# The block products of a fused attention kernel's projections change places, and loads within its attention are spread or moved behind it

## The chip, the cores and the metric

The kernel runs on one core of a Trainium2 chip. A core has a tensor engine (PE) for matrix products, a vector engine (DVE), a scalar engine (ACT), a general engine (POOL) and a queue engine (SP) from which nearly all transfers (DMA) are issued in order. Products go to PSUM, everything else lives in SBUF. The metric is the time of one execution on the device in microseconds. The kernel before took a median of 3309.8 us in three runs (3304.54 to 3311.78).

## The reference, cut to what matters

The input `x` is 8 images of 512 channels by 1024 positions, in float32. Two layers follow each other for each image:

```python
# layer 0, per image: 8 heads of 64 channels
hn  = group_norm(x, gn1)                       # 32 groups
q, k, v = split(w_qkv @ hn + b_qkv)
a   = softmax((q * s) @ (k * s)) @ v           # s = 64 ** -0.25, 1024 x 1024 per head
x1  = x + group_norm(w_proj @ a + b_proj, gn2)
# layer 1, per image: one head of 512 channels, weights normalized by rows
q, k, v = split(w1_qkv @ x1 / rms)             # rms over all 1536 channels of a position
h   = softmax(q.T @ k * 512 ** -0.5) @ v
out = (x1 + w1_out @ h) * 2 ** -0.5
```

Everything is computed in float32. The change touches layer 0 alone: the projections to q and k, and the loads that run during its attention.

## The kernel before, in words

**The loop.** `for b in range(B)` runs over the eight images, called batches here. In each, the attention of layer 0 has 32 steps: four pairs of heads (`j`), and for each pair eight blocks of 128 query rows. Step `i` does this, in `Heads.step`: the row maxima (DVE) and exponentials (ACT) of the scores made before; every second step the product of the probabilities with v (`values`, tile `po`) for two row blocks that lie some steps back; a piece of projection for the next pair (`fill`); the scores of step `i + 1` (`scores`, tile `s`); the transpose of the probabilities of step `i - 1` (`turn`: a DVE transpose from `p` to `pb`, then four transfers of 256 KB from `pb` to `pT`[...]); and the scaling of this step's probabilities on POOL (`scale`). What a step has in `later` follows at the end, among it the additions on POOL that belong to the projection piece (`due`, and those put off by a step, `rest`). So the scores of the first block of a pair are made at the end of the last step of the pair before, and need that pair's q and k by then. `pb`, `p` and the projected pairs `qk` have two buffers each, the scores three in PSUM, and the small products (`po` and the projection pieces) share two PSUM banks.

After the loop comes the drain: the last two `values`, the output projection with its weights `proj7`, the second group norm, and layer 1, which begins with a product with `gram` and reads `x`. In layer 1 the weights product has four units of seven products (`weight_unit`); the sums for the next batch's projection are made between them.

**The projection with seven products.** For pairs 1 to 3 of the batches 1 to 7 (21 times) q and k come from `project_seven`: q and k of both halves of the positions are a 2 by 2 block product, and are computed with seven block products in place of eight, as in Strassen's method in Winograd's form. The sums on the side of the activations are made once for each batch by `Sums`, in the tiles `t24` and `t31` (which lies in the buffer `v_`) and in `hn` itself; those on the side of the weights at the start by `operands_qk`, into `far["qk7"]` in DRAM, from which `fetch_qk` brings a pair's share (896 KB). Each block product is 64 rows deep in four chunks; those of the upper and the lower 64 rows run side by side on PE. `pieces` makes them in four pieces, one in every second step: the first with two chunks (the seventh product, divided over the two halves), the other three with four. ACT evacuates the two PSUM banks of a piece (to `q1`, `q2`, `k1`, `k2`, the halves of q and k, or to three temporaries `tmp`), and the list `adds` says what POOL adds after each piece, in the same step and one step later. For batch 0, and for pair 0 of each batch, `project_qk` or `project_rows` makes the eight products.

**Order.** `InOrder` keeps every instruction in the program's order on its engine; nothing is rescheduled. A step that waits holds up everything behind it on its engine. All instructions carry the line of that helper, so the profile is read by tiles. `Slots` hands out seven buffers of 16 KB a partition in the order in which they come free.

**Loads within attention.** With `i` the step, all on SP's queue between the transfers of `pT`: at 8 and 16 the weights of pair 3 and of the next batch's pair 0 (`fetch_qk`), at 21 `gram` (1 MB; in the last batch `proj`), at 24 `v` (1 MB, weights of layer 0), and at the ends of the steps 25 to 28 the four parts of `x` (512 KB each). `t24`, `gram` and `proj` share a buffer. POOL applies the first norm to the next batch's `hn` at the ends of the steps 1, 3, 5 and 7 (`norm1.apply`), in batches 1 to 6.

Of the kernel before, what the change touches and what calls it, by code (L numbers as in the profile page):

```python
# [10 lines left out]
AF = mybir.ActivationFunctionType  # L11
ALU = mybir.AluOpType
AX = mybir.AxisListType
P = 128
# [38 lines left out]
def attention_blocks_kernel(  # L53
# [29 lines left out]
    CI, NT, HN = C // P, N // P, N // 2  # L83
# [66 lines left out]
    def load_x(b, xt, ci):  # L150
        SY.dma_start(out=xt[:, ci, :], in_=xv[b, :, ci, :])
# [6 lines left out]
    rows = const.tile([GQKV, P], F32, name="rows")  # L158
# [31 lines left out]
    bkq = const.tile([P, CI], F32, name="bkq")  # L190
# [16 lines left out]
    def rsqrt(r, v, n, name):  # L207
# [43 lines left out]
    def fetch(name, b):  # L251
        SY.dma_start(out=place(name, b), in_=far[name])
# [98 lines left out]
    NB = N // P  # L351
    STEPS, LAG = CI * NB, 5
    halves = (slice(0, D), slice(D, P))
# [63 lines left out]
    class Sums:  # L417
# [2 lines left out]


        def __init__(self, b, hn):
            self.hn, self.t24, self.t31 = hn, place("t24", b), near["v_"].rearrange("p (ci n) -> p ci n", ci=CI)

        def steps(self):
            hn, t24, t31, (up, low) = self.hn, self.t24, self.t31, halves
            t1, t2 = slice(0, HN), slice(HN, N)
            SY.dma_start(out=t31[up], in_=hn[low, :, t2])
            yield
            for ci in range(CI):  # L430
                VE.tensor_sub(t31[up, ci], t31[up, ci], hn[up, ci, t2])
                yield
            for ci in range(CI):
                VE.tensor_add(t24[up, ci], t31[up, ci], hn[up, ci, t1])
                yield
            SY.dma_start(out=t24[low], in_=t24[up])
            for ci in reversed(range(CI)):
                VE.tensor_sub(hn[up, ci, t2], hn[up, ci, t2], hn[up, ci, t1])
                if ci == 2:
                    SY.dma_start(out=t31[low, :2], in_=hn[up, 2:, t2])  # L440
                yield
            for ci in range(CI):
                VE.tensor_sub(t24[low, ci], hn[low, ci, t1], t24[low, ci])
                yield

        def right(self, half, k):

            hn, t24, t31, rows = self.hn, self.t24, self.t31, halves[half]
            group, ci = divmod(k, CI)
            if group == 0:  # L450
                return hn[rows, ci, :HN]
            if group == 1:
                return t24[rows, ci]
            if half:
                return hn[rows, ci, HN:] if group == 2 else t31[rows, ci]
            return t31[rows, ci] if group == 2 else hn[rows, ci, HN:]

    def project_seven(b, j, right):

        qk = pair.tile([P, 2, N], F32, tag="qk", name=f"qk_{b}_{j}")
        kp = qk[:, 1, :].rearrange("p (be m) -> p be m", be=4)
        w, tmp = near["qk7"][:, (j - 1) % 2], [near["v#"][:, k * HN : (k + 1) * HN] for k in range(3)]

        def turned(t):
            return t.rearrange("p (m be) -> p be m", be=4)

        q1, q2 = (qk[:, 0, th * HN : (th + 1) * HN] for th in range(2))
        k1, k2 = (kp[:, :, th * P : (th + 1) * P] for th in range(2))  # L470

        def add(to, a, b_):
            return lambda: PO.tensor_add(to, a, b_)

        adds = (
            ([add(tmp[1], tmp[1], tmp[0])], []),
            ([], []),
            ([add(q2, q2, q1), add(k1, k1, turned(q2))], [add(q1, q1, tmp[0]), add(tmp[1], tmp[1], q2)]),
            ([add(k1, k1, k2), add(k2, k2, turned(tmp[1]))], [add(q2, tmp[1], tmp[2])]),
        )  # L480

        def pieces():
            for n, group in enumerate((3, 0, 1, 2)):
                pms = [bank(f"pq7_{b}_{j}_{n}_{r}") for r in range(2)]
                lo, hi = CI * group, min(CI * group + CI, 14)
                for k in range(lo, hi):
                    for r in range(2):
                        PE.matmul(pms[r], w[halves[r], k, :], right(r, k), start=(k == lo), stop=(k == hi - 1))
                if n == 0:
                    AC.copy(tmp[1], pms[0])  # L490
                elif n == 1:
                    AC.activation(q1, pms[0], AF.Identity, bias=bqs[:, j : j + 1])
                elif n == 2:
                    AC.copy(q2, pms[0])
                else:

                    AC.activation(k2, turned(pms[0]), AF.Identity, bias=bkq[:, j : j + 1])
                AC.copy(*((tmp[0], pms[1]), (tmp[0], pms[1]), (k1, turned(pms[1])), (tmp[2], pms[1]))[n])
                yield adds[n]

        return qk, pieces()
# [193 lines left out]
    class Seven:  # L695
# [8 lines left out]
        half, drains = None, []  # L704
# [310 lines left out]
    gram = place("gram", 0)  # L1015
# [6 lines left out]
    def operands_qk():  # L1022

        (up, low), q, k = halves, near["qk"][:, 0], near["qk"][:, 1]
        s = big("s_qk", 2 * CI)
        s1, s2 = s[up, :CI, :], s[:, CI:, :]
        s3 = block.tile([P, CI, C], F32, tag="pb", name="s3_qk")[up]
        SY.dma_start(out=far["qk0"], in_=near["qk"][:, :, :, :P])
        SY.dma_start(out=s1, in_=k[low])
        PO.tensor_add(s1, k[up], s1)  # L1030
        PO.tensor_sub(s2[up], s1, q[up])
        PO.tensor_sub(s3, q[up], k[up])
        SY.dma_start(out=s2[low], in_=s2[up])
        PO.tensor_sub(s2[low], q[low], s2[low])
        for rows, lo, hi, src in (
            (slice(0, P), 0, 4, q), (low, 4, 8, k[low]), (up, 4, 8, s2[up]), (up, 8, 12, s3), (up, 12, 14, s1[:, :2]),
            (low, 12, 14, s1[:, 2:]), (low, 8, 12, s2[low]),
        ):
            SY.dma_start(out=far["qk7"][rows, lo:hi, :], in_=src[:, :, P:])

# [34 lines left out]
    norm1 = Norm1(0, x0)  # L1075
# [22 lines left out]
    woT, proj = done2[:, :CI, :], done2[:, CI:, :]  # L1098
# [43 lines left out]
    heads, norm1, hn_next = Heads(0, x0, v0_0, qk0), None, None  # L1142
# [3 lines left out]
    for b in range(B):  # L1146
        hn, more = heads.hn, b + 1 < B
        todo, due, rest = iter(()), [], []
        for i in range(STEPS):
            j, r = divmod(i, NB)  # L1150
# [10 lines left out]
            early, later = [], []  # L1161
            if i < CI:
                fill, later = fills[i] + fill, laters[i]
# [9 lines left out]
                        todo = project_out_half(b, heads, o_last)  # L1173
            later.append(lambda: [f() for f in due])

            if b and more and i % 2 and i < 2 * CI:
                later.append(lambda: norm1.apply(i // 2, PO))
            if not b:


                if i == CI:
                    hn_next = big(f"hn_{b + 1}")
                    norm1 = Norm1(b + 1, hn_next)
# [15 lines left out]
                fetch_qk(CI - 1, b)  # L1199
            if b and i == 2 * NB and more:  # L1200
                fetch_qk(CI, b)
            if b and i == STEPS - NB - 3:
                fetch("gram" if more else "proj", b)
            if b and i == STEPS - NB and more:
                near["v"] = near["v_"].rearrange("p (ci c) -> p ci c", ci=CI)
                SY.dma_start(out=near["v"], in_=far["v"])

            if i == STEPS - NB + 1:
                xt = big(f"x_{b}")
            if 0 <= i - (STEPS - NB + 1) < CI:  # L1210
                later.append(lambda: load_x(b, xt, i - (STEPS - NB + 1)))
            heads.step(i, fill, early, later)

        if more:
# [4 lines left out]
        heads.turn()  # L1219
        if more:  # L1220
            fetch("proj7", b)
            ta = big(f"ta_{b}").rearrange("p (k i) (h n) -> p k i h n", k=2, h=2)
            rhs = RightSide(heads.a, ta[:, 0], ta[:, 1])
            for j in range(CI // 2 + 1):
                rhs.sums(j)
            for _ in range(3):
                next(v0)
        else:
            fetch("score", b)
            begun = OutBegun(b, heads)  # L1230
        heads.values(STEPS // RG - 1)
        slots.give(f"v0_{b}")
        if more:
# [84 lines left out]
```

## Time and profile before

| what | before |
|---|---|
| median of three runs | 3309.8 us (3304.54 to 3311.78) |
| profiled execution: time, span | 3305.3 us, 3303.5 us |
| PE busy (matmul) | 3242.3 us, 98% |
| DVE, POOL, ACT busy | 2235.7, 1129.4, 1064.0 us |
| granted PE clock | 0.997 |
| transfers `pb` to `pT` | 1024 of 256 KB, 4.6 us to landing (median) |
| attention of batch 2 (908 to 1090 us) | PE busy 176.2, DVE 147.1, POOL 109.1, ACT 92.8 us; DMA 0.79 busy, 214 GB/s |

The profile is of one execution. Busy times are sums of instructions of an engine; a matmul's end is modelled. A wait is written "engine tile <- releasing engine tile": the idle time of the first before an instruction on its tile, and who ended it. A name such as `po<-pT,v` is a group of instructions that write `po` and read `pT` and `v`. In the profile's names `tmp` appears as `v` (it lies in the same buffer as v), `t31` too, and `tt` are the reciprocal row sums.

### The profile page before, as it was taken

What the parts mean: (1) busy time and instruction counts of PE and PEld (TensorE: products, weight loads), DVE (VectorE), ACT (ScalarE), POOL (GpSimd) and SP (SyncE); (2) the same over time, 40 slices, a digit from 0 to 9 for tenths busy, and PEclk for the clock granted to TensorE, in tenths of its full rate; (3) what the DMA queues carried; (4) which work ended last, traced back from release to release, by engine and by line L of the source; (5) the groups of instructions that cost most, each with busy time, mean ns of one, the idle gap of its engine ahead of it and who ended that gap; (6) DMA issues with size and microseconds to landing.
All of it is one profiled execution on the core that took longest, in us unless ns stands there. A gap on an engine that the chain in (4) does not pass through costs nothing.

```text
span 3303.5 us, 35734 instructions
## 1 busy us (share of the span) xinstructions
PE 3242.3 (98%) x13010; PEld 1597.1 (48%) x13010; DVE 2235.7 (68%) x2982; ACT 1064.0 (32%) x1813; POOL 1129.4 (34%) x945
## 2 busy tenths in 40 slices
PE   8999999999999999999999999999999999999899
PEld 5444544445444454444544445444454445444354
DVE  5696667855688556885668756686566866668653
ACT  2453114521155211551215412254122531245210
POOL 0552125611266012650227503264033631246111
PEclk9999999999999999999999999999999999999899
DMA  6775216852178412783128812388114862057500
GB/s 188 217 199 166 75 37 172 223 152 58 48 190 230 137 35 65 201 237 102 45 77 208 244 67 49 100 211 235 62 53 109 223 192 74 16 153 205 183 7 26
DMA packets 227542, 435.22 MB, mean 132 GB/s; under 512 B 28484, under 2 KB 68968, under 8 KB 221288
## 3 DMA queue, kind: packets, MB, share of 16 engines
q1 hardware_dynamic: 227248, 432.91, 46.7%
q8 instruction: 104, 1.70, 0.2%
q14 instruction: 70, 0.57, 0.1%
q10 hardware_dynamic: 120, 0.02, 0.0%
HBM read 125.46 MB, written 28.74 MB: 47 GB/s over the span
## 4 chain that ended last, share of the span: by engine, by line
PE 84%; POOL 5%; DMA 3%; DVE 3%; SPq 2%; ACT 1%; issue 1%; DVEq 0%; ACTq 0%; POOLq 0%
PE po L34 22%; PE s L34 11%; PE p_e_T L34 7%; PE pv L34 7%; PE p_e_B L34 5%; PE pq L34 4%; PE py L34 4%; PE pqk L34 3%; PE p_u_T L34 3%; PE p_v_T L34 3%; DMA pT<-pb 3%; PE p_o_T L34 3%; PE p_v_B L34 3%; PE p_u_B L34 2%; POOL p L34 2%; PE p_o_B L34 2%
## 5 line engine op out<-in xcount | busy, mean ns | idle before, releaser
L34 ACT ACTIVATE p<-s,nm 128x1024 f32<-128x1024 f32 x512 | 565.5, 1109 | 919.0 <-DVE nm L34 800.8
L34 POOL TENSOR_SCALAR p<-p,tt 128x1024 f32<-128x1024 f32 x512 | 565.9, 1118 | 851.8 <-DVE tt L34 833.2
L34 DVE TENSOR_REDUCE nm<-s 128x1 f32<-128x1024 f32 x512 | 601.7, 1216 | 165.3 <-PE s L34 164.8
L34 DVE STREAM_TRANSPOSE pb<-p 128x2048 f32<-128x2048 f32 x256 | 590.0, 2305 | 79.1 <-DMA pT<-pb 53.3
L34 PE MATMUL s<-qk 64*128 64x512 f32 x2048 | 529.6, 604 | 26.0 <-POOL qk L34 25.1
L34 PE MATMUL po<-pT,v 128*64 128x256 f32 x4096 | 473.0, 384 | 9.4 <-DMA pT<-pb 9.2
L34 PE MATMUL po<-e,v 128*128 128x512 f32 x1024 | 451.7, 595 | 0.0
L34 PEld LDWEIGHTS po<-pT,v 128*64 128x64 f32 x4096 | 287.8, 137 | 232.2 <-ACT v L34 62.9
L34 POOL TENSOR_TENSOR u<-u,xy 128x512 f32<-128x512 f32 x64 | 79.0, 1275 | 769.3 <-DMA xy<-far_rinv 277.0
L34 PEld LDWEIGHTS s<-qk 64*128 64x128 f32 x2048 | 199.9, 186 | 282.0 <-issue 223.5
L34 PEld LDWEIGHTS po<-e,v 128*128 128x128 f32 x1024 | 191.9, 190 | 245.0 <-issue 236.4
L34 PE MATMUL pv<-v,hn 128*128 128x512 f32 x512 | 229.0, 598 | 0.0
L34 PE MATMUL pq<-hn,qk 64*128 64x512 f32 x588 | 191.2, 590 | 0.0
L34 POOL TENSOR_TENSOR esum<-esum,e 128x512 f32<-128x512 f32 x96 | 132.9, 1386 | 151.6 <-ACT e L34 149.0
L34 ACT ACTIVATE e<-e,shift,rinv 128x512 f32<-128x512 f32 x128 | 100.9, 812 | 256.3 <-DVE e L34 256.3
L34 PE MATMUL pqk<-hn,qk 64*128 64x512 f32 (+1 forms) x672 | 163.3, 590 | 0.0
L34 DVE TENSOR_TENSOR e<-e,p_e_T 128x512 f32<-128x512 f32 x160 | 107.0, 685 | 80.3 <-PE p_e_T L34 77.9
L34 PEld LDWEIGHTS pv<-v,hn 128*128 128x128 f32 x512 | 94.6, 190 | 115.1 <-issue 114.7
L34 PE MATMUL p_e_T<-s,t 128*128 128x512 f32 x320 | 147.8, 592 | 0.0
L34 PE MATMUL py<-x,gram 128*128 128x512 f32 x320 | 140.6, 599 | 6.0 <-issue 6.0
L34 PE MATMUL p_e_B<-u,x 128*128 128x512 f32 x256 | 116.4, 592 | 0.0
L34 ACT COPY v<-pv 128x1024 f32<-128x1024 f32 x32 | 32.2, 1007 | 259.5 <-PE pv L34 250.0
(208 smaller groups left out, 3773.8 us busy)
## 6 DMA issues: line engine op xcount, KB each, us to landing
pT<-pb SPq DMA_DIRECT2D x1024, 256.0 KB, 4.6
qk<-far_qk SPq DMA_DIRECT2D x21, 896.0 KB, 5.8
hn<-in_x_dram SPq DMA_DIRECT2D x32, 512.0 KB, 5.4
x<-in_x_dram SPq DMA_DIRECT2D x32, 512.0 KB, 6.0
out_dram<-x SPq DMA_DIRECT2D x32, 512.0 KB, 5.0
score<-far_score SPq DMA_DIRECT2D x8, 1792.0 KB, 7.5
value<-far_value SPq DMA_DIRECT2D x8, 1792.0 KB
proj<-far_proj SPq DMA_DIRECT2D x7, 1792.0 KB
```

The lines of the kernel that those rows point to most:

```text
L34: return lambda *args, **kw: self._pin(call(*args, **kw))
```

## The change

The three pieces of four chunks change places and contents, and so do the operands. Now the first piece has the two halves of the product that reads the second half of `hn` (after subtraction), the second and third give k1, k2, q1 and q2 their main parts, and the last piece has two products that are added to q alone. `adds` is written anew: k is complete after the third piece's additions, one step later; after the last piece the first addition is `q1 += tmp[0]`, then `q2 += tmp[1]`, and one step later `q2 += tmp[2]`. `Sums` makes the operands in another order and with one more copy within the chip, and three empty places before its last subtractions. `operands_qk` stores the weights in the new order.

Of the loads, `gram` goes behind the loop, after `proj7`; `v` is loaded in two halves at the steps 24 and 26; two parts of `x` are loaded at the steps 28 and 30, the other two behind the loop. The buffer of `x` is taken at step 28. POOL's `norm1.apply` stands at the steps 1, 2, 9 and 10.

```diff
@@ class Sums: steps
-            SY.dma_start(out=t31[up], in_=hn[low, :, t2])
+            SY.dma_start(out=t3[up], in_=hn[low, :, t2])
             yield
             for ci in range(CI):
-                VE.tensor_sub(t31[up, ci], t31[up, ci], hn[up, ci, t2])
+                VE.tensor_sub(t24[up, ci], t3[up, ci], hn[up, ci, t2])
                 yield
-            for ci in range(CI):
-                VE.tensor_add(t24[up, ci], t31[up, ci], hn[up, ci, t1])
-                yield
-            SY.dma_start(out=t24[low], in_=t24[up])
+            SY.dma_start(out=t3[low], in_=t24[up])
             for ci in reversed(range(CI)):
                 VE.tensor_sub(hn[up, ci, t2], hn[up, ci, t2], hn[up, ci, t1])
                 if ci == 2:
-                    SY.dma_start(out=t31[low, :2], in_=hn[up, 2:, t2])
+                    SY.dma_start(out=hn[low, :2, t2], in_=hn[up, 2:, t2])
                 yield
+            for ci in range(CI):
+                VE.tensor_add(t24[up, ci], t24[up, ci], hn[up, ci, t1])
+                yield
+            SY.dma_start(out=t24[low], in_=t24[up])
+            yield
+            yield
+            yield
             for ci in range(CI):
                 VE.tensor_sub(t24[low, ci], hn[low, ci, t1], t24[low, ci])
                 yield
+        def right(self, half, n, k):
+            rows = halves[half]
+            if n == 0 or (n, half) in ((1, 0), (3, 1)):
+                return self.hn[rows, k, HN:] if n == 0 else self.hn[rows, k, :HN]
+            return (self.t24 if n + half == 2 else self.t3)[rows, k]
@@ project_seven
         adds = (
             ([add(tmp[1], tmp[1], tmp[0])], []),
             ([], []),
-            ([add(q2, q2, q1), add(k1, k1, turned(q2))], [add(q1, q1, tmp[0]), add(tmp[1], tmp[1], q2)]),
-            ([add(k1, k1, k2), add(k2, k2, turned(tmp[1]))], [add(q2, tmp[1], tmp[2])]),
+            ([add(q2, q2, q1), add(k2, k2, turned(q2))], [add(k1, k1, k2), add(k2, k2, turned(tmp[1]))]),
+            ([add(q1, q1, tmp[0]), add(q2, q2, tmp[1])], [add(q2, q2, tmp[2])]),
         )
...
-            for n, group in enumerate((3, 0, 1, 2)):
+            for n in range(4):
...
                 if n == 0:
                     AC.copy(tmp[1], pms[0])
+                    AC.copy(tmp[0], pms[1])
                 elif n == 1:
                     AC.activation(q1, pms[0], AF.Identity, bias=bqs[:, j : j + 1])
+                    AC.copy(k1, turned(pms[1]))
                 elif n == 2:
                     AC.copy(q2, pms[0])
+                    AC.activation(k2, turned(pms[1]), AF.Identity, bias=bkq[:, j : j + 1])
                 else:
-                    AC.activation(k2, turned(pms[0]), AF.Identity, bias=bkq[:, j : j + 1])
-                AC.copy(*((tmp[0], pms[1]), (tmp[0], pms[1]), (k1, turned(pms[1])), (tmp[2], pms[1]))[n])
+                    AC.copy(tmp[0], pms[1])
+                    AC.copy(tmp[2], pms[0])
                 yield adds[n]
@@ operands_qk (stores of the weights)
-            (slice(0, P), 0, 4, q), (low, 4, 8, k[low]), (up, 4, 8, s2[up]), (up, 8, 12, s3), (up, 12, 14, s1[:, :2]),
-            (low, 12, 14, s1[:, 2:]), (low, 8, 12, s2[low]),
+            (up, 0, 2, s1[:, :2]), (low, 0, 2, s1[:, 2:]), (up, 2, 6, q[up]), (low, 2, 6, k[low]), (up, 6, 10, s2[up]),
+            (low, 6, 10, s3), (low, 10, 14, q[low]), (up, 10, 14, s2[low]),
@@ the steps of attention
-            if b and more and i % 2 and i < 2 * CI:
-                later.append(lambda: norm1.apply(i // 2, PO))
+            if b and more and i in (1, 2, 9, 10):
+                later.append(lambda: norm1.apply((1, 2, 9, 10).index(i), PO))
...
-            if b and i == STEPS - NB - 3:
-                fetch("gram" if more else "proj", b)
-            if b and i == STEPS - NB and more:
+            if b and i == STEPS - NB - 3 and not more:
+                fetch("proj", b)
+            m, odd = divmod(i - STEPS + NB, 2)
+            if b and more and m in (0, 1) and not odd:
                 near["v"] = near["v_"].rearrange("p (ci c) -> p ci c", ci=CI)
-                SY.dma_start(out=near["v"], in_=far["v"])
-            if i == STEPS - NB + 1:
+                SY.dma_start(out=near["v"][:, 2 * m : 2 * m + 2], in_=far["v"][:, 2 * m : 2 * m + 2])
+            if i == STEPS - 4:
                 xt = big(f"x_{b}")
-            if 0 <= i - (STEPS - NB + 1) < CI:
-                later.append(lambda: load_x(b, xt, i - (STEPS - NB + 1)))
+            if m in (2, 3) and not odd:
+                load_x(b, xt, m - 2)
@@ behind the loop
             fetch("proj7", b)
+            if b:
+                fetch("gram", b)
...
+        for ci in (2, 3):
+            load_x(b, xt, ci)
         heads.values(STEPS // RG - 1)
```

More of the change, by code (lines that the diff above doesn't have):

```diff
@@ L422, in __init__ @@
         def __init__(self, b, hn):
-            self.hn, self.t24, self.t31 = hn, place("t24", b), near["v_"].rearrange("p (ci n) -> p ci n", ci=CI)
+            self.hn, self.t24, self.t3 = hn, place("t24", b), near["v_"].rearrange("p (ci n) -> p ci n", ci=CI)
         def steps(self):
-            hn, t24, t31, (up, low) = self.hn, self.t24, self.t31, halves
+            hn, t24, t3, (up, low) = self.hn, self.t24, self.t3, halves
             t1, t2 = slice(0, HN), slice(HN, N)
-            SY.dma_start(out=t31[up], in_=hn[low, :, t2])
+            SY.dma_start(out=t3[up], in_=hn[low, :, t2])
             yield
             for ci in range(CI):
-                VE.tensor_sub(t31[up, ci], t31[up, ci], hn[up, ci, t2])
+                VE.tensor_sub(t24[up, ci], t3[up, ci], hn[up, ci, t2])
                 yield
-            for ci in range(CI):
-                VE.tensor_add(t24[up, ci], t31[up, ci], hn[up, ci, t1])
-                yield
-            SY.dma_start(out=t24[low], in_=t24[up])
+            SY.dma_start(out=t3[low], in_=t24[up])
             for ci in reversed(range(CI)):
@@ L444, in steps @@
                 yield
[L446 to L456, printed above, removed]
+        def right(self, half, n, k):
[3 more added lines that the diff above has]
+            return (self.t24 if n + half == 2 else self.t3)[rows, k]
     def project_seven(b, j, right):
@@ L477, in project_seven @@
             ([], []),
-            ([add(q2, q2, q1), add(k1, k1, turned(q2))], [add(q1, q1, tmp[0]), add(tmp[1], tmp[1], q2)]),
-            ([add(k1, k1, k2), add(k2, k2, turned(tmp[1]))], [add(q2, tmp[1], tmp[2])]),
+            ([add(q2, q2, q1), add(k2, k2, turned(q2))], [add(k1, k1, k2), add(k2, k2, turned(tmp[1]))]),
+            ([add(q1, q1, tmp[0]), add(q2, q2, tmp[1])], [add(q2, q2, tmp[2])]),
         )
         def pieces():
-            for n, group in enumerate((3, 0, 1, 2)):
+            for n in range(4):
                 pms = [bank(f"pq7_{b}_{j}_{n}_{r}") for r in range(2)]
-                lo, hi = CI * group, min(CI * group + CI, 14)
-                for k in range(lo, hi):
+                count, at = (CI, CI * n - 2) if n else (2, 0)
+                for k in range(count):
                     for r in range(2):
-                        PE.matmul(pms[r], w[halves[r], k, :], right(r, k), start=(k == lo), stop=(k == hi - 1))
+                        PE.matmul(pms[r], w[halves[r], at + k, :], right(r, n, k), start=(k == 0), stop=(k == count - 1))
                 if n == 0:
                     AC.copy(tmp[1], pms[0])
+                    AC.copy(tmp[0], pms[1])
                 elif n == 1:
                     AC.activation(q1, pms[0], AF.Identity, bias=bqs[:, j : j + 1])
+                    AC.copy(k1, turned(pms[1]))
                 elif n == 2:
                     AC.copy(q2, pms[0])
+                    AC.activation(k2, turned(pms[1]), AF.Identity, bias=bkq[:, j : j + 1])
                 else:
-                    AC.activation(k2, turned(pms[0]), AF.Identity, bias=bkq[:, j : j + 1])
-                AC.copy(*((tmp[0], pms[1]), (tmp[0], pms[1]), (k1, turned(pms[1])), (tmp[2], pms[1]))[n])
+                    AC.copy(tmp[0], pms[1])
+                    AC.copy(tmp[2], pms[0])
                 yield adds[n]
```

## The prediction

> **What bounds the kernel now.** I read first the busy shares, then the waits of the tensor engine (PE), then the timeline where a wait repeats. PE is busy for 98% of the span, but such busy time is modelled, so I looked for its gaps.
>
> ```profile
> PE 3242.3 (98%) x13010; PEld 1597.1 (48%) x13010; DVE 2235.7 (68%) x2982; ACT 1064.0 (32%) x1813; POOL 1129.4 (34%) x945
> ...
> PE s L34 <- POOL qk L34: 25.1, 21, 1.4
> PE po L34 <- DMA pT<-pb: 9.2, 7, 3.4
> ...
> DVE pb L34 <- DMA pT<-pb: 53.3, 39, 3.5
> ```
>
> The columns of a wait are total us, times and longest. PE's largest wait is on POOL for `qk`: 21 times, which is seven batches (1 to 7) by three pairs of heads (1 to 3) that `project_seven` makes. The next is the transposed probabilities `pT` that come late by DMA; DVE too waits for that DMA, because its transpose writes one of two `pb` buffers and the buffer is free only once its four transfers have been read out.
>
> The timeline shows the first wait in batch 2, at the change from pair 0 to pair 1 (columns: start us, length us, engine, operation, and in brackets the idle time before it):
>
> ```profile
> 945.81 0.68 ACT L34 ACTIVATE qk<-pq,bkq 128x512 f32<-128x512 f32 x1
> 946.16 1.20 POOL L34 TENSOR_SCALAR hn<-hn,a,c 128x1024 f32<-128x1024 f32 x1
> 946.80 0.12 DVE L34 RECIPROCAL tt<-tt 128x2 f32<-128x2 f32 x1
> 947.33 2.22 POOL L34 TENSOR_SCALAR p<-p,tt 128x1024 f32<-128x1024 f32 x2
> 947.35 3.67 PE L34 MATMUL po<-pT,v 128*64 128x256 f32 x32
> 949.50 1.29 POOL L34 TENSOR_TENSOR qk<-qk 128x512 f32<-128x512 f32 x1
> 950.88 1.51 POOL L34 TENSOR_TENSOR qk<-qk,v 128x512 f32<-128x512 f32 x1
> 952.45 1.99 PE L34 MATMUL s<-qk 64*128 64x512 f32 x8 [1.42 <-POOL qk L34]
> ...
> 990.97 3.67 PE L34 MATMUL po<-pT,v 128*64 128x256 f32 x32
> 992.81 1.28 POOL L34 TENSOR_TENSOR qk<-qk 128x512 f32<-128x512 f32 x1
> 994.17 1.52 POOL L34 TENSOR_TENSOR qk<-qk,v 128x512 f32<-128x512 f32 x1
> 995.75 1.99 PE L34 MATMUL s<-qk 64*128 64x512 f32 x8 [1.10 <-POOL qk L34]
> ```
>
> Step 6 evacuates the final piece of the pair; POOL scales the step's probabilities (two instructions), then adds twice into k; PE, done with `po`, stands until the second add has ended (950.88 + 1.51 = 952.39, scores at 952.45). For pair 1 the `hn` instruction of POOL makes it 0.3 us worse.
>
> The second wait, at the end of the attention of batch 2:
>
> ```profile
> 1078.71 2.31 DVE L34 STREAM_TRANSPOSE pb<-p 128x2048 f32<-128x2048 f32 x1 [1.39 <-DMA pT<-pb]
> 1088.91 3.67 PE L34 MATMUL po<-pT,v 128*64 128x256 f32 x32 [1.59 <-DMA pT<-pb]
> ```
>
> The transpose of row block 29 ends at 1081.0; its transfers have landed only at 1088.9, 7.9 us later, where the median is 4.6 us. In front of them on the queue stood the loads of this stage: `gram` (1 MB, step 21), `v` (1 MB, step 24), `x` (four of 512 KB, steps 25 to 28).
>
> **What the Trainium skill says.** "Perfetto Trace Analysis", Identifying the Most-Contended Engine, says that matmul busy share doesn't show how near PE is to its limit; here 98% busy goes with gaps that add up. The same page, Optimization Strategy, says to take the gaps of the busiest engine, find who releases them, and let that dependency start sooner: the POOL row above is such a gap. "DMA: Bandwidth & Descriptors", Issuing engines are not separate DMA queues, says that all DMAs run on the same 16 engines and interleave; the trace agrees, since `pT` lands in 7.9 instead of 4.6 us behind loads that have nothing to do with it.
>
> **The change, part by part.** *Final piece.* PE has the same 28 small products for each pair, 4 + 8 + 8 + 8, so nothing is added there. ACT has the same six copies and two biased activations; they change pieces (the third one's pair gets 0.09 us longer: 684 against 593 ns), before a `po` group whose bank is free some 0.4 us early (copies end at 936.21, `po` at 936.68): nothing. POOL has the same eight additions for each pair. What changes is which ones the next pair's scores need: before, two k additions of the last piece; after, only `q1 += tmp[0]`, the first of that step. The built program's order confirms it: the scores wait for the first of those two additions, not for the second nor for the one a step later. With the times of pair 2: POOL's scaling ends at 992.81, the addition takes 1.28, so q is ready at 994.09, and with 0.06 us from POOL to PE (952.39 to 952.45) at 994.15. PE is free 3.60 us after 990.97 (an undisturbed `po` group, 936.68 to 940.28), at 994.57. The margin is 0.42 us. For pair 1, `norm1.apply` leaves steps 3, 5 and 7 for 2, 9 and 10: the scaling can begin when the reciprocal is there (946.80 + 0.12 + some 0.1 = 947.03), ends at 949.2, the addition at 950.5; PE is free at 950.95. So all 25.1 us go. *What is late next:* the scores of the next pair come 1.1 to 1.4 us earlier, and behind them the reduce, exponentials and copies; DVE stood 2.4 us idle there waiting for PE, so the chain moves as one piece. The 1.16 us that PE then loses at the next `po` (955.98 to 958.95: 2.97 us for eight matmuls at 0.215 = 1.72, less the 0.1 usual at this switch), because the short piece of four products gives PE less than DVE and ACT need for a step, stays.
>
> *Loads.* `gram` goes behind the last `pT` and `proj7`, where only `py`, tens of us later, needs it; `x` keeps two of four loads, at steps 28 and 30, the others go to the drain; `v` becomes two halves at steps 24 and 26. So 4 MB in eight steps become 2 MB, never more than 512 KB in two steps. Measured cover: in batch 0 (four x loads, one each step, no gram, no v) and in batch 7 after step 23 (same), the waits of DVE for `pb` between step 23 and step 30 are nil; in batches 1 to 6 they come to 9.5, 12.3, 10.1, 5.8, 6.7 and 6.2 us from step 21 on. What of it reached PE I take from starts in the timeline, against batch 0: steps 24 to 30 longer by 1.5, 1.9, 2.0, 1.1, 1.3, 0.3 us (8.1), and the first `po` after the loop late by 1.7, 1.9 and 0.7 us in batches 2, 3 and 6 (4.3). Together 12.4 us; bounds 0 and 12.4, I take 10. SP's queue: each moved load still stands between two groups of `pT` issues, and none waits for something younger than PE's reads of two steps before, so nothing is held up behind them; in the drain no `pT` follows.
>
> *The sums of `hn`.* The same 16 DVE instructions and one copy of 512 KB more (four in place of three), in the weight products, where PE shows no gap. The chain is longer: the last t24 transfer is issued some 4.8 us later (at about 844.6 against 839.8 in batch 1), the subtractions that need it some 6 us after that, and such a copy within the chip took 4.7 us. Hidden; if not, DVE would stand up to 1 us, with two products (3.4 us) of PSUM in hand.
>
> *What may be lost.* At step 8 the fetch of 896 KB of weights stands in front of `pT`; DVE waited for it 0.8, 1.5 and 0.2 us in batches 4, 5 and 7 and PE lost nothing. With scores earlier by 1.2 us these transfers have that much less time. Bounds 0 and 1 us for each of seven batches; I take 2 us. In batch 7 a load at step 21 (`proj`) stays, and DVE starts the transpose of step 22 2.35 us late (3040.67; the profile names POOL's `qk`, which this instruction doesn't read, and the probabilities were scaled at 3037.7, so I take it to be the `pb` transfers). So far that lay under PE's own wait for POOL; without the cover 0 to 1.2 us, I take 0.5. The order of the set-up stores is free: the last of them waits for the same subtraction.
>
> Sum: -25.1 - 10 + 2 + 0.5 = -32.6 us. The profiled execution took 3305.3 us (span 3303.5), so it would take 3272.7; the median of the runs shown is 4.5 us above that execution, so the median goes to 3277.
>
> **Rivals.** *Only POOL's wait goes:* the load at step 30 stands directly in front of `pT` 29, which the first `po` after the loop needs, and keeps it as late as now. For: the queue is in order and in that stage DMA is 0.8 to 0.9 busy. Against: only 0.5 MB in two steps. -25 + 2.5 + 2 gives 3289. *The wait moves to DVE and DMA:* DVE is busy 147 of 182 us of this stage; if the 1.2 us that PE gains at each pair are lost again at the next `po`, about half of the 25 us is left and little of the loads: 3298. Against: DVE's idle of 2.4 us at this very place. *The change doesn't do it:* if PE went on waiting for two additions (by POOL being late: a margin of 0.42 us, below half of one addition), the 25 us stay and only the loads give 7 to 10: 3301. *Slower:* the fetch at step 8. It is on the queue of `pT`, and takes some 3.5 us at the 250 to 290 GB/s seen there. If it held DVE by more than the 1.5 us that PE has been seen to bear, everything above comes out of PE once per pair; to use up 33 us it would have to cost 4.7 us in each of seven batches, three times the longest wait seen there. From about 5 us on the kernel is slower: 3317.
>
> **Chances.** Forecast 0.64, only POOL's wait 0.17, moved wait 0.09, change without effect 0.03, slower 0.04, and 0.03 for no difference. What a measurement of this kernel can tell from no change is about 0.2%, 6.6 us (3303.2 to 3316.4). The forecast's own range is 3266 to 3286; with the first rival and part of the second the range is 3263 to 3299. Faster 0.91, same 0.05, slower 0.04.
>
> **What would show it.** Right: "PE s waits for POOL qk" goes from 25.1 us to under 3; between the transposes of steps 22 and 30 DVE's wait for `pT` falls from the 50 us of the six sums above to under 10; the `po` after the loop has no wait for DMA. Wrong: a new wait of PE on ACT or DVE of about 1 us at the first or second `po` of each pair, or a wait of DVE for `pT` above 2 us at the transposes of steps 9 and 30. A margin below 0.42 us in the rows of POOL and PE would make the forecast wrong at its largest term.

## The result, and the profile after

The changed kernel takes 3268.9 us (median of four runs, 3267.05 to 3270.34), the kernel before 3307.2 us (four runs, 3304.08 to 3311.78). The ratio is 0.9883, with a 95% interval of 0.9866 to 0.9900: 38.3 us less. The profiled execution took 3268.6 us, with a span of 3266.5 us against 3303.5.

First the same views as before. Of the kernel after, the busy shares and the shares of the chain that ended last, from the page:

```profile
PE 3235.1 (99%) x13010; PEld 1597.2 (49%) x13010; DVE 2229.7 (68%) x2982; ACT 1064.6 (33%) x1813; POOL 1127.6 (35%) x945
...
PE 90%; DMA 4%; DVE 3%; SPq 2%; issue 1%; POOL 0%; DVEq 0%; ACT 0%; ACTq 0%; POOLq 0%
```

Of the kernel before, the shares of the same chain:

```profile
PE 84%; POOL 5%; DMA 3%; DVE 3%; SPq 2%; ACT 1%; issue 1%; DVEq 0%; ACTq 0%; POOLq 0%
```

The busy times hardly move: the work is the same. What moves is the chain: POOL had 5% of it and now has none.

The waits of the kernel after, those of PE and of DVE (total us, times, longest):

```profile
PE py L34 <- issue: 6.0, 1, 6.0
PE pG L34 <- DVE w_qk L34: 5.5, 1, 5.5
PE po L34 <- DMA pT<-pb: 4.9, 5, 2.6
```

```profile
DVE pb L34 <- DMA pT<-pb: 24.6, 17, 3.4
```

PE's largest wait, 25.1 us on POOL for `qk`, is gone altogether; `po` on DMA has gone from 9.2 to 4.9 us, and DVE's wait for the buffer `pb` from 53.3 to 24.6 us. The two that now stand on top occur once, and were there before.

The timeline of the kernel after, in batch 2, at the changes from pair 0 to pair 1 and from pair 1 to pair 2:

```profile
943.76 2.52 POOL L34 TENSOR_TENSOR qk<-qk,v 128x512 f32<-128x512 f32 x2
945.52 1.99 PE L34 MATMUL s<-qk 64*128 64x512 f32 x8
...
985.19 3.67 PE L34 MATMUL po<-pT,v 128*64 128x256 f32 x32
987.14 2.51 POOL L34 TENSOR_TENSOR qk<-qk,v 128x512 f32<-128x512 f32 x2
988.79 1.99 PE L34 MATMUL s<-qk 64*128 64x512 f32 x8
```

The scores have no idle time before them. POOL's two additions stand in one row; the first, on which the scores now wait, takes 1.28 us of it and ends at 988.42, and PE is free at 988.79, which is 3.60 us after its `po` began. The margin is 0.37 us here. In 18 of the 21 places it is 0.48 us, and the smallest is 0.13. The end of the attention of the same batch after, with the transpose of row block 29 and the first `po` behind the loop:

```profile
1067.22 2.30 DVE L34 STREAM_TRANSPOSE pb<-p 128x2048 f32<-128x2048 f32 x1
...
1077.23 3.67 PE L34 MATMUL po<-pT,v 128*64 128x256 f32 x32
```

Neither waits for transfers; before, they stood 1.39 and 1.59 us.

Two places are worse. The timeline after, in batch 2 where the weights of pair 3 are loaded, and in the last batch behind the load of `proj`:

```profile
949.81 1.20 SPq L34 DMA_DIRECT2D qk<-far_qk  x1
...
962.62 2.31 DVE L34 STREAM_TRANSPOSE pb<-p 128x2048 f32<-128x2048 f32 x1 [2.62 <-DMA pT<-pb]
962.96 3.67 PE L34 MATMUL po<-pT,v 128*64 128x256 f32 x32 [0.19 <-DMA pT<-pb]
...
3005.82 2.31 DVE L34 STREAM_TRANSPOSE pb<-p 128x2048 f32<-128x2048 f32 x1 [3.21 <-DMA pT<-pb]
```

For a balance I take PE's time from the starts of its groups in the timeline, in us. "Over the usual" is what a stretch takes more than in the batches in which nothing is late:

| where PE's time lies | before | after | difference |
|---|---|---|---|
| first scores of a pair (end of steps 7, 15, 23 of batches 1 to 7), over the usual | 26.5 | 0 | -26.5 |
| steps 24 to 30 of batches 1 to 6, over the usual | 8.1 | 0 | -8.1 |
| from the last scores of batches 1 to 6 to the first `po` behind the loop, over the usual | 5.4 | 1.2 | -4.2 |
| steps 11 to 13 of batches 1 to 7, over the usual | 0.1 | 2.6 | +2.5 |
| step 25 of the last batch, over the usual | 0.1 | 1.4 | +1.3 |
| last batch, from its last scores to its last `po` | 20.7 | 18.2 | -2.5 |
| all the rest | | | +0.5 |
| span | 3303.5 | 3266.5 | -37.0 |

From the last `po` of the batches 1 to 5 to their first product with `gram`, and from there to the next batch's first scores, both traces take the same 41.92 and 151.82 us. So neither the loads that went behind the loop nor the longer chain of `Sums` costs anything there.

### The profile page after: what moved, and what is told of

It is laid out like the page before. It is cut to its first block, busy times and chain, and to the rows that moved or that the text cites. A ratio compares the mean times of both kernels' runs of the same rounds, so it can differ in the third digit from the quotient of the medians.

```text
span 3266.5 us, 35730 instructions
## 1 busy us (share of the span) xinstructions
PE 3235.1 (99%) x13010; PEld 1597.2 (49%) x13010; DVE 2229.7 (68%) x2982; ACT 1064.6 (33%) x1813; POOL 1127.6 (35%) x945
## 4 chain that ended last, share of the span: by engine, by line
PE 90%; DMA 4%; DVE 3%; SPq 2%; issue 1%; POOL 0%; DVEq 0%; ACT 0%; ACTq 0%; POOLq 0%
PE po L34 25%; PE s L34 12%; PE pv L34 7%; PE p_e_T L34 7%; PE pq L34 6%; PE p_e_B L34 5%; PE py L34 4%; PE pqk L34 4%; DMA pT<-pb 4%; PE p_u_T L34 3%; PE p_v_T L34 3%; PE p_o_T L34 3%; PE p_v_B L34 3%; PE p_u_B L34 3%; PE p_o_B L34 2%; DVE pb L34 2%
## 5 line engine op out<-in xcount | busy, mean ns | idle before, releaser
L34 DVE STREAM_TRANSPOSE pb<-p 128x2048 f32<-128x2048 f32 x256 | 589.8, 2304 | 42.6 <-DMA pT<-pb 24.6
L34 POOL TENSOR_TENSOR qk<-qk,v 128x512 f32<-128x512 f32 x124 | 162.8, 1320 | 3.2 <-ACT v L34 1.6
L34 PE MATMUL pq<-t,qk 64*128 64x512 f32 x336 | 150.9, 589 | 0.0
L34 PE MATMUL pq<-v,qk 64*128 64x512 f32 x336 | 150.9, 589 | 0.0
```

The lines of the kernel that those rows point to most:

```text
L34: return lambda *args, **kw: self._pin(call(*args, **kw))
```

## The experiments

The theory was the prediction's sum: POOL's wait and the late transfers are two separate amounts, and small losses remain at two loads. The rivals ask which part gave the time, whether the order of two additions decides as claimed, and what sets the losses. Ratios are to the kernel before on the same chip.

**The projection alone.** The changed kernel with the loads and `norm1.apply` where they were.

```diff
-            if b and more and i in (1, 2, 9, 10):
-                later.append(lambda: norm1.apply((1, 2, 9, 10).index(i), PO))
+            if b and more and i % 2 and i < 2 * CI:
+                later.append(lambda: norm1.apply(i // 2, PO))
...
-            if b and i == STEPS - NB - 3 and not more:
-                fetch("proj", b)
-            m, odd = divmod(i - STEPS + NB, 2)
-            if b and more and m in (0, 1) and not odd:
+            if b and i == STEPS - NB - 3:
+                fetch("gram" if more else "proj", b)
+            if b and i == STEPS - NB and more:
                 near["v"] = near["v_"].rearrange("p (ci c) -> p ci c", ci=CI)
-                SY.dma_start(out=near["v"][:, 2 * m : 2 * m + 2], in_=far["v"][:, 2 * m : 2 * m + 2])
+                SY.dma_start(out=near["v"], in_=far["v"])
...
+            if 0 <= i - (STEPS - NB + 1) < CI:
+                later.append(lambda: load_x(b, xt, i - (STEPS - NB + 1)))
...
```

> The new block products, sums and stored weights alone; all loads and the norm's places on POOL as before. Theory (two separate causes, POOL's additions worth 26 us and the loads worth 10 to 12): 25 to 28 us faster than the kernel before, PE's wait on POOL for qk gone or under 2 us, since even with the hn instruction in step 5 the first addition ends some 0.1 us before PE is free; DVE's waits for pT at the end of the attention stay near 50 us. Rival (the old place of the norm's instructions or the loads bring the wait back): less than 18 us faster. Rival (the loads matter more once POOL's wait no longer covers them): less than 24 us, with new waits of PE in steps 23 to 25.

Measured: 3292.5 us, ratio 0.9959 (0.9946 to 0.9973), so 14.7 us less than before, and not 25. The waits of this kernel:

```profile
PE po L34 <- DMA pT<-pb: 5.2, 7, 1.6
...
PE s L34 <- POOL qk L34: 1.8, 7, 0.5
```

```profile
DVE pb L34 <- DMA pT<-pb: 69.8, 50, 3.8
```

POOL's wait is gone but for one of 0.5 us in batch 4 and some 0.3 us at the end of step 7 in batches 1 to 6 (1.8 us together). Batch 7, which has no `norm1.apply`, has none of the latter, so these 1.8 us are what moving it is worth; no run moves it alone. Yet DVE waits for transfers 69.8 us, more than the 53.3 of before. Its timeline in batch 2 shows where:

```profile
1054.46 2.31 DVE L34 STREAM_TRANSPOSE pb<-p 128x2048 f32<-128x2048 f32 x1 [3.82 <-DMA pT<-pb]
1054.68 3.67 PE L34 MATMUL po<-pT,v 128*64 128x256 f32 x32 [1.28 <-DMA pT<-pb]
...
1071.48 2.31 DVE L34 STREAM_TRANSPOSE pb<-p 128x2048 f32<-128x2048 f32 x1 [2.70 <-DMA pT<-pb]
```

In steps 24 to 30 of batches 1 to 6 PE now loses 15.1 us where it lost 8.1, and in steps 11 to 15 it loses 4.4 where it lost 0.1 (2.7 of them in batch 4 alone). So -26.5 + 1.8 + 7.0 + 4.3 = -13.4 us, of the 13.9 by which the span of this trace is shorter. That is the second rival; the first one's bound of 18 us is met too, but its reason, POOL's wait coming back, is worth 1.8 us only.

The transfers came late in the kernel before too, and POOL's wait covered part of it. This can be read at step 25, which has 5.0 of the 7.0 us. In this trace the transposes of step 22 are late by 2.82, 2.06, 2.14, 2.67, 0.62 and 3.10 us in batches 1 to 6, and step 25 is longer by 1.35, 0.59, 0.67, 1.19, 0 and 1.63: PE bears 1.47 us of lateness and loses what goes beyond. Before, these transposes were late by 1.7 to 2.8 us, and step 25 lost 0.5 us in all six batches together; there PE's wait of 1.17 us for POOL at the end of step 23 lay between.

**The loads alone.** The kernel before with the loads of the kernel after; projection and `norm1.apply` as before.

```diff
-            if b and i == STEPS - NB - 3:
-                fetch("gram" if more else "proj", b)
-            if b and i == STEPS - NB and more:
+            if b and i == STEPS - NB - 3 and not more:
+                fetch("proj", b)
+            m, odd = divmod(i - STEPS + NB, 2)
+            if b and more and m in (0, 1) and not odd:
...
-            if 0 <= i - (STEPS - NB + 1) < CI:
-                later.append(lambda: load_x(b, xt, i - (STEPS - NB + 1)))
+            if m in (2, 3) and not odd:
+                load_x(b, xt, m - 2)
...
+            if b:
+                fetch("gram", b)
...
```

> The moved and split loads alone; projections and the norm's places on POOL as before. Theory: 10 to 13 us faster (the steps 24 to 30 of batches 1 to 6 shorter by 8 us in sum, the first po after the loop by 3 to 4); PE's wait on POOL stays at 25 us; DVE's waits for pT at the transposes of steps 22 to 30 go. Rival (the loads are hidden as long as POOL's wait gives them cover): under 4 us.

Measured: 3294.1 us, ratio 0.9962 (0.9950 to 0.9975), 13.1 us less. The waits of this kernel, PE's and DVE's:

```profile
PE s L34 <- POOL qk L34: 26.9, 21, 3.0
```

```profile
DVE pb L34 <- DMA pT<-pb: 14.7, 12, 3.0
```

POOL's wait stays whole, with its 21 occurrences; the late transfers go, and steps 24 to 30 are at their usual times in every batch. One gap of 3.5 us in batch 4 occurs once and isn't in the other traces. The four corners, as us of median (and of the span in the profiled execution) against the kernel before:

| | loads as before | loads as after |
|---|---|---|
| projection as before | 0 | -13.1 (-9.0) |
| projection as after | -14.7 (-13.9) | -38.3 (-37.0) |

The parts give 27.8 us one by one and 38.3 together. The last corner has the moved `norm1.apply` besides (1.8 us), so about 8.7 us come only when both are done. In the medians that is near what their intervals allow (each some 5 us wide to either side); the trace shows it directly, by the 7.0 us that appear in steps 24 to 30 when POOL's wait goes and the loads stay.

**The order of the last two additions.** The changed kernel with two additions swapped, so that the scores wait for the second.

```diff
-            ([add(q1, q1, tmp[0]), add(q2, q2, tmp[1])], [add(q2, q2, tmp[2])]),
+            ([add(q2, q2, tmp[1]), add(q1, q1, tmp[0])], [add(q2, q2, tmp[2])]),
```

> The changed kernel with the two POOL additions of the last piece in the other order, so that the scores of the next pair wait for the second addition instead of the first; no instruction more or less. Theory (POOL's second addition of 1.3 to 1.5 us is the whole wait): 22 to 27 us slower than the changed kernel, that is 11 to 16 us faster than the one before; PE's wait on POOL for qk back at about 1.1 to 1.2 us in each of 21 places. Rival (the gain came from k being ready earlier, or from the norm's move): within 5 us of the changed kernel.

Measured: 3286.3 us, ratio 0.9939 (0.9925 to 0.9952), some 17 us slower than the changed kernel. PE's wait is back, 21 times, in the waits and at pair 2 of batch 2 in the timeline of this kernel:

```profile
PE s L34 <- POOL qk L34: 16.0, 21, 1.0
```

```profile
988.07 3.67 PE L34 MATMUL po<-pT,v 128*64 128x256 f32 x32
989.93 2.51 POOL L34 TENSOR_TENSOR qk<-qk,v 128x512 f32<-128x512 f32 x2
992.49 1.99 PE L34 MATMUL s<-qk 64*128 64x512 f32 x8 [0.75 <-POOL qk L34]
```

That the first addition alone decides is shown. The size was expected too high, because I took the 1.1 to 1.4 us from the kernel before, where the second addition reads `tmp` turned, with a stride, and takes 1.52 us; here it takes 1.28. From the start of the first addition to the end of the second it is 2.51 us against 2.88 before (992.81 to 995.69), and the wait is 0.75 against 1.10.

**`gram` at step 21 again.** The changed kernel with this load alone put back.

```diff
-            if b and i == STEPS - NB - 3 and not more:
-                fetch("proj", b)
+            if b and i == STEPS - NB - 3:
+                fetch("gram" if more else "proj", b)
...
-            if b:
-                fetch("gram", b)
```

> The changed kernel with the load of gram (1 MB) at step 21 again, in batches 1 to 6; all else as changed. Theory (this load makes the transpose of step 22 some 2.5 us late, which POOL's wait used to cover and now nothing covers, as in the last batch, whose step 25 lost 1.3 us): 6 to 9 us slower than the changed kernel, with DVE's wait for pT back at step 22 and PE losing 1 to 1.5 us at step 25 of each of the six batches. Rival (PE bears 2.5 us as it bore 1.5 at step 9): under 2 us.

Measured: 3275.2 us, ratio 0.9906 (0.9890 to 0.9921), 6.3 us slower than the changed kernel; the intervals overlap, so the trace has to carry it. DVE in batch 2 of this kernel, at the transpose of step 22, and its sum of waits:

```profile
1033.44 2.31 DVE L34 STREAM_TRANSPOSE pb<-p 128x2048 f32<-128x2048 f32 x1 [2.30 <-DMA pT<-pb]
```

```profile
DVE pb L34 <- DMA pT<-pb: 53.4, 41, 3.5
```

The transposes of step 22 are late by 2.57, 2.30, 1.57, 2.06, 0.46 and 3.00 us in batches 1 to 6, in the kernel after by nothing. Step 25 is longer by 1.10, 0.82, 0.10, 0.59, 0 and 1.53 us: again PE bears 1.47 us and loses what goes beyond. The span is 8.5 us longer: 4.4 in steps 24 to 30 of batches 1 to 6, 1.5 at the first `po` behind the loop, and some 1.8 in steps 7 to 13 and 0.7 in the last batch, which this edit doesn't explain. So one load of 1 MB, needed only tens of us later, is worth about 6 us by its place.

**The weights of pair 3 in two halves.** The changed kernel; in place of 896 KB at step 8, half at step 10 and half at step 12.

```diff
-            if b and i == NB:
-                fetch_qk(CI - 1, b)
+            if b and i in (NB + 2, NB + 4):
+                k = 7 * (i == NB + 4)
+                SY.dma_start(
+                    out=near["qk7"][:, CI % 2, k : k + 7], in_=far["qk7"][:, k : k + 7, (CI - 2) * P : (CI - 1) * P]
+                )
```

> The changed kernel with the 896 KB of pair 3's weights loaded in two halves at steps 10 and 12 instead of whole at step 8. Theory (this load is what made the transposes of step 9 late by 0.5 to 2.6 us in all of batches 1 to 7 and cost PE 2 to 3 us in steps 11 to 13): 2 to 3 us faster than the changed kernel, DVE's wait at step 9 gone, step 13 back to its 0.24 us in each batch. Rival (the transfers of pT are late there in any case, since the short step leaves them less time): no difference, the wait stays.

Measured: 3267.3 us, ratio 0.9887 (0.9870 to 0.9903). The same place in batch 2 of this kernel:

```profile
959.62 2.30 DVE L34 STREAM_TRANSPOSE pb<-p 128x2048 f32<-128x2048 f32 x1
959.86 1.13 SPq L34 DMA_DIRECT2D qk<-far_qk  x1
962.40 3.67 PE L34 MATMUL po<-pT,v 128*64 128x256 f32 x32
```

The transpose that stood 2.62 us doesn't stand, and steps 11 to 13 are at their usual times in all batches, as they are in the two further runs with these halves. In the five traces that have the new projection and the load whole these steps lose between 1.5 and 4.1 us in sum. So the load at step 8 was the cause; whether its halving or its later place removes the loss was not separated. The time doesn't show it: the span falls by 1.1 us only, since the set-up before the first scores and the drain of the last batch are 1.2 and 1.3 us longer in this execution.

**`proj` in halves as well.** The kernel of the last paragraph, with `proj` in two halves at steps 21 and 26 of the last batch.

```diff
-            if b and i == STEPS - NB - 3 and not more:
-                fetch("proj", b)
+            if b and not more and i in (STEPS - NB - 3, STEPS - NB + 2):
+                k = 2 * (i == STEPS - NB + 2)
+                to = near["proj"] if k else place("proj", b)
+                SY.dma_start(out=to[:, k : k + 2], in_=far["proj"][:, k : k + 2])
```

> As the run with the spread weights of pair 3, and in the last batch proj in two halves at steps 21 and 26 instead of whole at step 21. Theory: 1 to 1.5 us faster than that run, since the last batch's step 25 loses 1.3 us to a late transpose of step 22; in sum 3 to 4.5 us faster than the changed kernel. Rival: as that run.

Measured: 3267.4 us, ratio 0.9887 (0.9872 to 0.9902). In the last batch of this kernel:

```profile
3001.51 2.31 DVE L34 STREAM_TRANSPOSE pb<-p 128x2048 f32<-128x2048 f32 x1 [0.31 <-DMA pT<-pb]
```

It stood 3.21 us in the kernel after. But in the run before this one, with `proj` whole, it was:

```profile
3002.72 2.31 DVE L34 STREAM_TRANSPOSE pb<-p 128x2048 f32<-128x2048 f32 x1 [1.13 <-DMA pT<-pb]
```

In the eight traces with `proj` whole this transpose is 1.1 to 3.5 us late, in the two with halves 0.3 us and not at all. So the halves take the lateness away. PE's loss at step 25 is another matter: PE bears 1.8 us at this place, so step 25 had its usual time in the run before already, and this pair of runs doesn't show that the halves win it. As a time nothing is won (3267.4 against 3267.3 us; 1 to 1.5 were expected).

**The copies before the second exponential.** The changed kernel; at steps 8 and 16 ACT evacuates the short piece (two copies) before the second exponential, and not after it. It asks whether the 1.16 us that stay at steps 9 and 17 wait for these copies, which free the banks of `po`.

```diff
...
+                if hold and hh:
+                    self.held = exp
+                else:
+                    exp()
...
-            self.softmax(i)
+            self.held = None
+            self.softmax(i, bool(self.b) and i in (NB, 2 * NB))
...
+            if self.held:
+                self.held()
```

> The changed kernel with another order on ACT in the steps 8 and 16 of batches 1 to 7: the two evacuations of the short first piece stand between the step's two exponentials, not behind both; no instruction more or less. Theory as predicted (the short piece gives PE less than DVE and ACT need for a step, so the 1.16 us at the next po stays in one form or another): within 3 us of the changed kernel, the wait moved by a step. Rival (po waits for its PSUM bank only because the evacuations stand behind the second exponential, and DVE has 0.8 us to spare there): 8 to 15 us faster, the 1.4 us at steps 9 and 17 down to about 0.5.

Measured: 3270.0 us, ratio 0.9895 (0.9880 to 0.9910): no difference to the changed kernel. Its timeline in batch 2 (PEld is the weight load of PE):

```profile
948.80 1.11 ACT L34 ACTIVATE p<-s,nm 128x1024 f32<-128x1024 f32 x1 [2.75 <-DVE nm L34]
949.00 3.04 PE L34 MATMUL s<-qk 64*128 64x512 f32 x8
949.91 1.06 ACT L34 COPY v<-pq 128x512 f32<-128x512 f32 x2
950.06 0.30 PEld L34 LDWEIGHTS s<-qk 64*128 64x128 f32 x4 [0.87 <-ACT p L34]
951.97 3.67 PE L34 MATMUL po<-pT,v 128*64 128x256 f32 x32
```

The copies end at 950.97 in place of 952.12, and `po` starts as late as ever, 2.97 us after the scores; steps 9 and 17 have 1.40 us in every batch, as in the kernel after. The banks of `po` are not the cause. The row of the weight load says what is: the scores of the second head wait for ACT's first exponential. The three score buffers are used two for each step, so that the second head of step 9 needs the one that the exponential of step 8's first head frees, at 948.80 + 1.11 = 949.91; from 950.06 on PE goes at its usual pace. "Perfetto Trace Analysis" of the Trainium skill, Optimization Strategy, says that the same gap repeated over a stretch can mean that SBUF or PSUM has no room for the next tile; this gap of 1.16 us, at the same step of every batch, fits that. No run had another number of score buffers (the three with two banks each and the two small banks are all that the kernel's PSUM holds), so the attribution is read from the timeline and was not tried.

**All three together.** The changed kernel with both loads in halves and the early copies.

> The spread weights of pair 3, the spread proj of the last batch and the earlier evacuations together, on top of the changed kernel. If both sets of theories hold: 3 to 7 us faster than the changed kernel; with the rival on the evacuations 11 to 19 us faster.

Measured: 3266.0 us, ratio 0.9884 (0.9870 to 0.9899). DVE's wait of this kernel:

```profile
DVE pb L34 <- DMA pT<-pb: 3.8, 8, 0.9
```

DVE waits for nearly no transfer any more, and the span is 2.5 us shorter than that of the kernel after. But by its ratio to the kernel before (0.9884, the changed kernel has 0.9883) the time is that of the changed kernel, and the 3 to 7 us expected are not shown.

## Why the prediction was right, and where its sizes were off

The forecast was 3277 us with 3266 to 3286 as its own range; it took 3268.9. About half of these 8 us has nothing to do with the change: the prediction added 4.5 us, by which the median before lay above the profiled execution, and after the two lie only 0.3 us apart. By its steps:

*Final piece, -25.1.* Right, at -26.5, and the swapped additions confirm that the first of them decides. The margin of 0.42 us counted 0.06 from POOL to PE; counted in this way it came to 0.31 at the same place, and to 0.07 at the tightest. The prediction had named a margin below 0.42 as a sign that its largest term is wrong. That sign was set too strictly, for PE waited at none of the 21 places. The chain behind it moved as one piece, as said: the rival by which the gain is lost again at the next `po` (3298) is refuted, since steps 8, 9, 16 and 17 take exactly what they took.

*Loads, -10.* Of the right size and undersized: -8.1 and -4.2, close to the bound of 12.4. The reading behind the second part was incomplete. By the starts of PE's groups the first `po` was late by 1.7, 1.9, 0.3 and 0.7 us in batches 2, 3, 4 and 5, and the last scores of batch 1 by 0.8, together 5.4 and not 4.3. Another reading put unlike times side by side: the 7.9 us run from the end of a transpose to the landing of the last of its four transfers, the 4.6 us from the issue of one transfer. The last of those four was issued at 1083.68 and landed at 1088.67, 5.0 us later; over the stretch from 1031 to 1090 us the median was 5.5. So behind the loads a transfer took about 1 us longer than usual and not 3.3, and the `po` was late mostly because the transpose had itself started 1.39 us late. Of the signs named, DVE's is there: between the transposes of steps 22 and 30 its wait is nil in batches 1 to 6, and at step 30 too. "The `po` after the loop has no wait for DMA" is not wholly met: it waits 0.31 us in batch 1 and 0.74 in batch 4, and in the last batch, whose drain is another, 2.62 and 0.99 us.

*The addition of the two terms.* The sum holds for both edits together. The loads alone are worth what was taken for them and more (13.1 us), but the projection alone gives 14.7 and not 25, since behind POOL's wait the same transfers were late. The prediction knew this cover for one load ("so far that lay under PE's own wait for POOL; without the cover 0 to 1.2 us") and didn't ask the same of the others. The first rival (POOL's wait alone goes, 3289) has its counterpart in the projection alone, 3292.5; it did not come true because the loads moved too, and those at steps 28 and 30 kept nothing late.

*The sums of `hn`.* Nothing, as said: the stretch in which they are made has the same length before and after.

*Step 8, +2.* Right in size: +2.5, in batches 1, 2, 3 and 6. A sign that the prediction named for being wrong, a wait of DVE above 2 us at the transpose of step 9, is there in batches 1 and 2 (2.48 and 2.62 us), but PE lost only 1.0 and 1.1 us for it, what goes beyond some 1.5 here too. That the size fits is partly luck, since other traces with the load whole have 1.5 to 4.1. The two halves at steps 10 and 12 remove the loss, so the cause is shown. It is far from the 4.7 us in each batch at which the slower rival would decide.

*Last batch, +0.5.* Undersized: +1.3, just over the upper bound of 1.2; the transpose there was late by 3.21 us, not by the 2.35 seen under POOL's wait.

*The sum.* -32.6 was forecast for the execution, and the span fell by 37.0: 1.4 and 2.3 us more from the two large terms, 1.3 less for the two losses, 2.5 from the drain of the last batch, which no step had, and 0.5 the other way in the rest. Over the ten traces the last batch takes 18.2 to 21.9 us from its last scores to its last `po`. The kernel after has the shortest of them, but with two additions swapped it is 20.3 and with the weights of pair 3 in halves 19.5, edits that touch nothing near it. So I count it as chance and not to the change.

*The 1.16 us that stay.* They stay, and the reason given, that PE has less to do there than DVE and ACT, fits what the timeline shows. The place was taken wrongly: PE doesn't stand at `po`, but within the scores before it, whose second head needs the buffer that ACT's first exponential frees.

## What to carry to other kernels

When the same engine has two waits close to each other in time, the first may give the second one's transfers time to arrive. Removing the first alone is then worth less than its length (14.7 us of 25 here), while removing both is worth the sum. So run each edit alone before saying what it gives, and look at what an existing wait covers before removing it. A late transfer costs nothing up to what the bounding engine can bear behind it, here some 1.5 us; compare its lateness with that before giving it a price. A load that only a later stage needs is worth moving out of the stretch where transfers on the same queue are awaited, even if no engine names it in its own waits.

## What the runs showed of the hardware

A load whose data are needed only later still sets the pace: with 896 KB of weights ahead of them, transfers from `pb` to `pT` held DVE for 2.62 us, and with the load in two halves, two and four steps later, for nothing. The 16 DMA engines were 0.82 and 0.83 busy in these two traces from 908 to 1090 us. And an addition of 128 by 512 on POOL took 1.28 us with no operand strided and 1.52 us with one read at a stride of four elements. These 0.24 us are most of the 0.37 by which the two additions of the swapped order (2.51) take less time than those of the kernel before (2.88).
